# Parking seven sets of weight factors in DRAM through GpSimd's DMA queue instead of SyncE's, in a two-layer graph kernel

## Chip, cores and metric

The kernel runs on one core of one Trainium2 chip. The metric is the device time of one execution in microseconds (us). Three runs of the kernel before took 2225.2, 2225.92 and 2229.39 us; the median is 2225.92 us.

## What is computed

The input is 128 graphs of 128 nodes with 512 features each, and a 128 x 128 adjacency matrix per graph. Two layers follow each other, both with a layer norm ahead of them and a residual sum behind them.

```python
h = jnp.maximum(_layernorm(x, axis=-1), 0.0)
x = x + _L0_gnn_ref(h, adj, ...)     # attention over the edges, then three hops:
    # transition = row-normalised A * exp(leaky_relu(...))
    # for k in range(3): H += Xk @ Wk[k] + bk[k]; Xk = transition @ Xk ; relu(H)
h = jnp.maximum(_layernorm(x, axis=-1), 0.0)
x = x + _L1_gnn_ref(h, adj, nodemask, ...)
    # q, k = split(h @ Wqk); v = h @ Wv; agg = adj @ k
    # softmax over the nodes of (q . agg) / sqrt(512), times v
```

Everything is float32.

## The kernel before

**Staging.** The graphs are taken in 64 pairs p. A first loop (`for p in range(NP)`, from line 745 on) does layer 0 for all pairs and prepares layer 1; a second part, from line 842 on, does layer 1 on quads of graphs. Products with weights are done by Strassen's scheme, with seven products in place of eight block products (`strassen`, line 371), in layer 1 by two nested levels of it.

**One pass of the first loop** has, on TensorE, the seven products of `y10(p)`, the eight small products of `inner(p)` and `outer(p)` that apply the attention matrix (tile `tt`), and the seven products of `y2(p + 2)`, which belong to a later pair. Around them run:

- `load_x(p + 4)` (line 101): SyncE's queue loads the input of a later pair into `xg`. VectorE takes its statistics one pass later (line 290), ScalarE its norm.
- `outer`, line 621 and 623: VectorE adds the residual into `x1`, and SyncE's queue stores that to `x1d`. 
- `t_by_blocks` (lines 529 and 534): the attention matrix goes to DRAM (`td`) and comes back in blocks (`tv`, printed as `junk`); VectorE transposes it into `tt` for the next pass.
- `norm2` with `by_blocks` (lines 337 and 342): the normed input of layer 1 goes to `h2d` and comes back by blocks as `hv`. `for_layer1`, in the next pass, transposes `hv` into `fw` (line 427). In the second pass of each two passes it then forms two sums of it on VectorE (lines 442 and 443); in the first pass, two sums of older data (its `upper`, ahead of the transposes). GpSimd's queue stores `fw` to `fd` (line 435).
- the end of `y2` (lines 470 and 472): GpSimd's queue stores a small transposed tile to `pzd` and, once that has landed, loads it back spread over all partitions as `pz`. `pz` is used in the next pass (`attention_exp`).
- `load_adj(p + 3)` (lines 107 and 111): one load on SyncE's queue and four on GpSimd's (`agb`).

**Weights for layer 1.** Layer 1's right-hand factors need the inner level of the scheme too. In the passes p = 9 to 15 (`FIRST` = 9, seven `FACTORS`), `prepare` makes one factor a pass: four VectorE subtractions of 128 x 256 elements into a `stage` tile (line 191; two of them in `between`, two in the middle of the statistics), and `store_all`, which puts seven blocks into the DRAM tile `RWD[o]`: the four of `stage` and three that are parts of the factor itself (`rl`, later `tl`). `rightl[o][:, k, h * HD:(h + 1) * HD]` is block (k, h) of that factor. In the passes p = 16 to 19, four of the seven are read back into `RW[o]`; the other three are read by GpSimd's queue after the loop.

**What sets the order.** Each engine executes its instructions in one order, and its queue issues its DMAs in one order with the waits in between. The order is set by a planner, which may place an instruction against its place in the program (in the trace the `agb` loads of a pass stand ahead of the store to `pzd` that the program makes first); `behind(what, op, ...)` puts an instruction behind a named one, `done[what]`, in the order of the same engine. `store_all` is put behind `x1d`, so on SyncE's queue the four stores stand right behind the store of `x1` and ahead of the next `load_x`. (Through such helpers many instructions carry line 86 in the profile; they are told apart by their tiles.)

Of the kernel before, what the change touches and what calls it, by code (L numbers as in the profile page):

```python
# [16 lines left out]
def kernel(  # L17
# [25 lines left out]
    nc = tc.nc  # L43
    B, N, D = x.shape
# [5 lines left out]
    G = 2  # L50
# [26 lines left out]
    done = {}  # L77
# [5 lines left out]
    def behind(what, op, *args, **how):  # L83

        with tc.issue_after(done[what]):
            return op(*args, **how)  # L86
# [6 lines left out]
    def bcast(ap, offset, n):  # L93

        return bass.AP(tensor=ap.tensor, offset=ap.offset + offset, ap=[[0, P], [1, n]])
# [100 lines left out]
    def combined(r, t):  # L196
        return dict(zip((5, 6, 7, 4, 1, 2, 3), t + [r[0, 0], r[1, 0], r[1, 1]]))
# [124 lines left out]
    HV, LEFT, Y2, PZ, T, TT, X1, HV2, FW = ({} for _ in range(9))  # L322
# [48 lines left out]
    def strassen(banks, left, right, s, first, ends, steps={}, gate="warm", second="warm", seventh="warm"):  # L371

        w = right[1].shape[2:]
        a, b, c, e = (t[:, :w[0]] if len(w) == 1 else t for t in banks)

        def product(bank, i, start=False):
            if len(w) > 1:
                bank = bank.rearrange("p (k o) -> p k o", k=w[0])  # L380
            for k in range(HC):
                ordered(nc.tensor.matmul, bank, left[i][:, k * P:(k + 1) * P], right[i][:, k],
                        start=(start and k == 0), stop=(k == HC - 1), skip_group_check=True)
            if i in steps:
                steps[i]()

        product(a, 1, first)
        done["ba"] = behind(second, nc.scalar.copy, b, a).ins
        product(e, 5, first)
        done["s"] = behind(gate, nc.scalar.copy, s[:, 0], e).ins  # L390
        product(b, 6)
        done["u2"] = behind("s", nc.scalar.copy, c, b).ins
        product(a, 2)
        ends[0, 0](a)
        product(c, 7)
        done["s7"] = behind(seventh, nc.scalar.copy, s[:, 1], c).ins
        ends[1, 1](e, s[:, 1])
        product(b, 3)
        ends[0, 1](b, s[:, 0])
        product(c, 4)  # L400
        ends[1, 0](c)
# [45 lines left out]
    def y2(p, steps={}, gate=None, after="ln"):  # L447


        add = partial(behind, gate, nc.vector.tensor_add) if gate else nc.vector.tensor_add  # L450
        y = Y2[p] = front.tile([P, G, 2, WP], FP, name="y2")[:, :, :, :W2]
        s = front.tile([P, 2, WP * 2], FP, name="s", bufs=1)[:, :, :W2]

        def y00(a):
            done["y00"] = behind(after if gate else "warm", nc.scalar.copy, y[:, 0, 0], a).ins

        def y10(c):
            done["y10"] = nc.scalar.copy(y[:, 1, 0], c).ins

        strassen(set2, LEFT[p], right2, s, True, {  # L460
            (0, 0): y00,
            (1, 1): lambda e, t: add(y[:, 1, 1], e, t),
            (0, 1): lambda b, t: add(y[:, 0, 1], b, t),
            (1, 0): y10}, steps, seventh="y00")
        if p > 1:

            t = small.tile([P, G, S32], FP, name="pzt", bufs=1)
            behind(gate or "warm", nc.vector.transpose, t, y[:, :, 0, :S32])
            d = dram.tile([G, Q, S32], FP, name="pzd")
            nc.gpsimd.dma_start(d.rearrange("g q b -> q g b"), t[::S32])  # L470
            PZ[p] = front.tile([P, G, N], FP, name="pz")
            nc.gpsimd.dma_start(PZ[p].rearrange("p g n -> p (g n)"), bcast(d, 0, G * N))
        else:
            PZ[p] = a2[:, :G * N].rearrange("p (g n) -> p g n", g=G)

# [167 lines left out]
    rightl = {}  # L643
    RWD = {o: dram.tile([P, 7, HD], FP, name=f"rwd{o}", bufs=1) for o in FACTORS}
# [4 lines left out]
    def prepare(o, stage):  # L649

        r = {(k, h): rightl[o][:, k, h * HD:(h + 1) * HD] for k in range(2) for h in range(2)}
        t = stage.tile([P, 4, HD], FP, name="stage")

        def store_all():
            behind("x1d", nc.sync.dma_start, RWD[o][:, :4], t)
            for i, at in enumerate(((0, 0), (1, 0), (1, 1))):
                behind("x1d", nc.sync.dma_start, RWD[o][:, 4 + i], r[at])

        return combine_steps(r, [t[:, i] for i in range(4)]), store_all

# [84 lines left out]
    for p in range(NP):  # L745
        weights, weights_end = [], None
        if DC < p <= 2 * DC:
            weights = combine_steps(*OUTER)[p - DC - 1:p - DC]
            weights_end = lambda: rightl.update(combined(*OUTER))
        elif FIRST <= p < FIRST + len(FACTORS):  # L750
            weights, weights_end = prepare(FACTORS[p - FIRST], stage)

        def between():
            if p == 0:
                behind("t", norm0, 2)
                behind("rs", begin, 1)
                return
            if len(weights) > 1:
                for step in weights[:2]:
                    behind("t", step)  # L760
            if p + 2 < NP:
                behind("right" if weights else "t", begin, p + 2)
            if p + 3 < NP:
                two = weights[-2:]
                RS0[p + 3] = behind("left", statistics, xg[p + 3],
                                    middle=(lambda: [behind("aggr", step) for step in two]) if two else None, last="right")

        if p == NP - 1:
            behind("rs2", attention, p)
        def norms():  # L770
            if p and p + 3 < NP:
                behind("s7", norm0, p + 3, RS0.pop(p + 3))

        steps = {1: between, 3: norms}
        if p in T:
            steps[2] = lambda: t_transposed(p)
        if p > 1:
            steps[5] = lambda: masked(p, "ba")
        y10(p, steps)
        if p > 0:  # L780
            behind("c12", for_layer1 if p < NP - 1 else SUMS.pop(NQ - 2), *([p - 1] if p < NP - 1 else []))
        if p == NP - 2:
            f0 = w2[:, :8 * G * HC * N].rearrange("p (o j k n) -> p o j k n", o=8, j=G, k=HC)
            load_left(0, swdge)
        if p == NP - 1:
            for step in inner_sums(0, FACTORS[:4]):
                behind("c12", step)
        z = inner(p)
        if p == 0:
            y2(1, {2: lambda: RS0.update({3: behind("left", statistics, xg[3], "u2")})})  # L790
            behind("y10", behind, "hv", norm0, 3, RS0.pop(3))
            spread_columns(1)
            attention(1, lambda: begin(2))
        behind("c12" if p else "left", outer, p, z)
        if weights:
            weights_end()
        if p + 4 < NP:
            load_x(p + 4)
        if 0 < p <= DC:
            behind("x1d", rows, rl[:, :, 1], wv1, (p - 1,))  # L800
        if p == 0:
            setup_ctx.close()
            left = layer0.enter_context(tc.tile_pool(name="left", bufs=1))
            stage_ctx = ExitStack()
            stage = stage_ctx.enter_context(tc.tile_pool(name="stage", bufs=2, side="right"))
        if p + 2 < NP:
            def ahead():
                attention_exp(p + 1, gate="aggr")
                attention_adj(p + 1)

            def statistics_and_ahead():
                norm2_statistics(p, middle=ahead)
                attention_t(p + 1, "rs2")
                t_by_blocks(p + 1)

            y2(p + 2, *(({2: statistics_and_ahead}, "t", "z") if p else ()))
        if p + 2 < NP:
            behind("s7", seed_a)
            behind("s7", seed_e)
        elif p + 1 < NP:  # L820
            seeds_last()
        norm2(p)
        if p + 3 < NP:
            load_adj(p + 3)
        if p == FIRST + len(FACTORS):
            stage_ctx.close()
            prep_ctx.close()
            early = ctx.enter_context(tc.tile_pool(name="early", bufs=1, side="right"))
            RW = {o: early.tile([P, 7, HD], FP, name=f"rw{o}") for o in FACTORS[:4]}
        if FIRST + len(FACTORS) <= p < FIRST + len(FACTORS) + 4:  # L830
            o = FACTORS[p - FIRST - len(FACTORS)]
            behind("x1d", nc.sync.dma_start, RW[o], RWD[o])
    def left1(q, o, i):
        if i in INNER:
            return IN[q, o][:, INNER[i]]
# [523 lines left out]
```

## Time and profile before

| What | Value |
|---|---|
| Median of three runs | 2225.92 us |
| The profiled execution, its own time | 2229.96 us |
| Its span, first to last instruction | 2228.2 us |
| TensorE (PE) busy | 2205.7 us, 99% of the span |
| VectorE (DVE) busy | 1672.1 us, 75% |
| ScalarE (ACT) busy | 1235.8 us, 55% |
| GpSimd (POOL) busy | 698.6 us, 31% |
| Mean granted TensorE clock | 0.999 |
| Stores to `rwd` on SyncE's queue (SPq) | 28, from 260.6 to 401.9 us |
| Loads `rw<-rwd` on SyncE's queue | 4, from 427.3 to 492.3 us |
| Loads `rw<-rwd` on GpSimd's queue | 3, from 1430.4 to 1431.4 us |

Matmul ends are modelled, so a busy TensorE says only that it was fed. Idle times of TensorE in a stretch, and the distance from one pass to the next, say more. In lists of instructions each row is: line, engine, operation, tiles written and read, count, durations in ns (least, median, most), first and last start. In lists of waits each row is: who waited, for whom, us in total, how often, the longest.

### The profile page before, as it was taken

The numbers are of one execution on the slowest core, as the hardware profiler recorded it, in microseconds if no ns is written. First come the engines' busy times: TensorE is split into PE (matmuls) and PEld (weight loads), VectorE is DVE, ScalarE is ACT, GpSimd is POOL, SyncE is SP. The second block draws the span as 40 slices with busy tenths as digits, with TensorE's granted clock in tenths as the row PEclk, the third lists the DMA queues.
The fourth block names the chain that finished last, engine by engine and source line by source line (L and its number), as shares of the span: only waits on it lengthen the run. The fifth ranks groups of instructions, "written<-read, shape, count | busy, mean of one in ns | idle before, by whom it ended". The sixth has DMA issues, their size and how long they took to land.

```text
span 2228.2 us, 29421 instructions
## 1 busy us (share of the span) xinstructions
PE 2205.7 (99%) x8113; PEld 1535.0 (69%) x8113; DVE 1672.1 (75%) x4529; ACT 1235.8 (55%) x2858; POOL 698.6 (31%) x822
## 2 busy tenths in 40 slices
PE   9999999999999999999999999999999999999998
PEld 5666665656666665666666666688888878887886
DVE  5778777778787777877778787587777767777777
ACT  4555554455554555545555554456666666666664
POOL 3111111111121211212112121245555555555454
PEclk9999999999999999999999999999999999999999
DMA  7688788888787887878778786668888888888876
GB/s 208 181 243 244 230 266 248 266 271 246 225 239 222 238 238 220 244 227 232 234 227 241 218 245 211 250 205 239 223 262 226 237 223 256 235 227 242 239 219 179
DMA packets 425615, 519.35 MB, mean 233 GB/s; under 512 B 100310, under 2 KB 281174, under 8 KB 409578
## 3 DMA queue, kind: packets, MB, share of 16 engines
q1 hardware_dynamic: 383880, 391.84, 58.1%
q0 software_dynamic: 41280, 125.09, 21.6%
q8 instruction: 65, 1.06, 0.2%
q14 instruction: 100, 0.82, 0.1%
q10 hardware_dynamic: 290, 0.53, 0.1%
HBM read 295.26 MB, written 222.07 MB: 232 GB/s over the span
## 4 chain that ended last, share of the span: by engine, by line
PE 90%; DVE 4%; DMA 3%; SPq 1%; ACT 1%; issue 1%; DVEq 0%
PE a L91 26%; PE c L91 24%; PE b L91 24%; PE e L91 15%; DMA td<-t 2%; DMA hv<-h2d 1%; SPq L534 1%; DVE st L290 0%; DMA tl<-in_L_gnn_Wqk_dram 0%; DVE fw L427 0%; DVE z L86 0%; SPq L342 0%; DVE x L621 0%; DMA xg<-in_x_dram 0%; SPq L86 0%
## 5 line engine op out<-in xcount | busy, mean ns | idle before, releaser
L669 POOL TENSOR_TENSOR c<-s,c 128x512 f32<-128x512 f32 (+1 forms) x186 | 201.0, 1094 | 250.2 <-DVE s L669 244.9
L111 POOL DMA_DIRECT2D agb<-in_adj_dram x256 | 149.7, 591 | 338.8 <-DVE aT L86 251.8
L91 PE MATMUL a<-r,x 128*128 128x512 f32 x512 | 242.4, 596 | 0.1
L91 PE MATMUL b<-rw,in 128*128 128x256 f32 x884 | 212.0, 379 | 0.0
L91 PEld LDWEIGHTS b<-rw,in 128*128 128x128 f32 x884 | 168.0, 190 | 23.3 <-issue 0.5
L435 POOL DMA_DIRECT2D fd<-fw x62 | 34.7, 559 | 464.3 <-DVE fw L443 278.0
L91 PEld LDWEIGHTS a<-r,x 128*128 128x128 f32 x512 | 97.6, 191 | 96.8 <-issue 93.4
L86 ACT COPY s<-c 128x257 f32<-128x257 f32 (+1 forms) x128 | 61.5, 481 | 173.4 <-PE c L91 173.2
L86 ACT COPY b<-a 128x257 f32<-128x257 f32 (+1 forms) x128 | 59.3, 464 | 171.6 <-PE a L91 171.6
L86 DVE TENSOR_TENSOR e<-e,s 128x512 f32<-128x512 f32 x64 | 44.7, 699 | 143.5 <-ACT s L86 143.5
L669 POOL TENSOR_TENSOR c<-c 128x1024 f32<-128x1024 f32 x61 | 144.1, 2362 | 11.2 <-DVE c L669 10.9
L91 PE MATMUL a<-w,x 128*128 128x257 f32 x512 | 131.9, 380 | 0.1
L91 PE MATMUL b<-w,sx 128*128 128x257 f32 x512 | 132.0, 380 | 0.0
L91 PE MATMUL b<-t,sx 128*128 128x512 f32 x256 | 120.4, 592 | 1.2 <-ACT b L86 1.2
L91 PE MATMUL c<-t,sx 128*128 128x512 f32 x256 | 120.5, 593 | 0.2
L91 PE MATMUL b<-r,sx 128*128 128x512 f32 x256 | 120.3, 592 | 0.0
L91 PE MATMUL e<-t,sx 128*128 128x512 f32 x256 | 120.3, 592 | 0.0
L91 PE MATMUL c<-t,x 128*128 128x512 f32 x256 | 120.3, 592 | 0.0
L669 DVE SCALAR_TENSOR_TENSOR junk<-agg,wscale,c 128x512 f32<-128x512 f32 x126 | 97.1, 770 | 29.9 <-POOL c L669 24.6
L669 ACT ACTIVATE c<-c,wcol 128x512 f32<-128x512 f32 x124 | 86.3, 720 | 56.7 <-DVE wcol L669 56.7
L427 DVE STREAM_TRANSPOSE fw<-hv 128x256 f32<-128x256 f32 x248 | 88.1, 413 | 30.1 <-DMA hv<-h2d 29.7
L91 PE MATMUL a<-rw,f 128*128 128x256 f32 x448 | 108.1, 379 | 0.0
(265 smaller groups left out, 5258.1 us busy)
## 6 DMA issues: line engine op xcount, KB each, us to landing
fd<-fw POOLq DMA_DIRECT2D x62, 1024.0 KB, 5.1
x1d<-x SPq DMA_DIRECT2D x64, 512.0 KB, 4.2
h2d<-h SPq DMA_DIRECT2D x64, 512.0 KB, 3.7
xg<-in_x_dram SPq DMA_DIRECT2D x63, 512.0 KB, 7.1
hd<-h SPq DMA_DIRECT2D x63, 512.0 KB, 3.6
hv<-hd SPq DMA_DIRECT2D x252, 128.0 KB, 4.2
hv<-h2d SPq DMA_DIRECT2D x248, 128.0 KB, 4.1
h<-h2d SPq DMA_DIRECT2D x62, 512.0 KB, 8.4
```

Source lines behind the costliest of these rows:

```text
L86: return op(*args, **how)
L91: done["mm"] = op(*args, **how).ins
L111: nc.gpsimd.dma_start(agb[p][c * S32:(c + 1) * S32].rearrange("p g q i -> p (g q) i"), v[c])
L427: done["c12"] = nc.vector.transpose(blocks[:, k, j].rearrange("p f (n b) -> p f n b", n=Q), hv[:, j].rearrange("p n (k f a) -> p k f n a", ...
L435: nc.gpsimd.dma_start(fd[:, half].rearrange("p o n -> p (o n)"), fv[:, half].rearrange("p o n -> p (o n)"))
L534: done["tv"] = nc.sync.dma_start(tv[c * S32:(c + 1) * S32].rearrange("p g q i -> p (g q) i"), v[c]).ins
L669: done[engine] = op(*args, **how).ins
```

## The change

The four stores a pass become three: the blocks (1, 0) and (1, 1) lie side by side in the factor, so one store takes both. All three go through GpSimd's queue, behind the load of `pz`, which gets a name in `done` for that. The call of `store_all` moves behind `y2(p + 2)` in the program, since that `pz` load is made there. The four loads back in the passes 16 to 19 go through GpSimd's queue too, behind `pz` as well. The data moved and VectorE's subtractions stay as they are.

```diff
-            nc.gpsimd.dma_start(PZ[p].rearrange("p g n -> p (g n)"), bcast(d, 0, G * N))
+            done["pzq"] = nc.gpsimd.dma_start(PZ[p].rearrange("p g n -> p (g n)"), bcast(d, 0, G * N)).ins
...
         def store_all():
-            behind("x1d", nc.sync.dma_start, RWD[o][:, :4], t)
-            for i, at in enumerate(((0, 0), (1, 0), (1, 1))):
-                behind("x1d", nc.sync.dma_start, RWD[o][:, 4 + i], r[at])
+            behind("pzq", nc.gpsimd.dma_start, RWD[o][:, :4], t)
+            behind("pzq", nc.gpsimd.dma_start, RWD[o][:, 4], r[0, 0])
+            behind("pzq", nc.gpsimd.dma_start, RWD[o][:, 5:7].rearrange("p i d -> p (i d)"), rightl[o][:, 1])
...
         behind("c12" if p else "left", outer, p, z)
-        if weights:
-            weights_end()
         if p + 4 < NP:
             load_x(p + 4)
...
             y2(p + 2, *(({2: statistics_and_ahead}, "t", "z") if p else ()))
+        if weights:
+            weights_end()
         if p + 2 < NP:
             behind("s7", seed_a)
...
             o = FACTORS[p - FIRST - len(FACTORS)]
-            behind("x1d", nc.sync.dma_start, RW[o], RWD[o])
+            behind("pzq", nc.gpsimd.dma_start, RW[o], RWD[o])
```

## The prediction, made before the result was known

> **What bounds the kernel now.** The page first: TensorE is busy nearly throughout, so only its idle time can be won.
>
> ```profile
> PE 2205.7 (99%) x8113; PEld 1535.0 (69%) x8113; DVE 1672.1 (75%) x4529; ACT 1235.8 (55%) x2858; POOL 698.6 (31%) x822
> ```
>
> Then busy time in stretches of 50 us (after the stretch: PE, PEld, DVE, ACT, POOL, each with its count, then granted clock, DMA share, GB/s), to see where TensorE idles.
>
> ```profile
> 150.00:200.00 50.00, 50.00 (x175) 32.96 (x174) 42.31 (x133) 27.62 (x66) 10.95 (x19) 1.00 0.86 255
> ...
> 250.00:300.00 50.00, 48.92 (x161) 30.17 (x160) 38.38 (x117) 25.56 (x59) 8.14 (x14) 1.00 0.82 246
> 300.00:350.00 50.00, 47.96 (x158) 30.10 (x157) 37.29 (x120) 24.16 (x57) 8.69 (x15) 0.97 0.86 267
> 350.00:400.00 50.00, 47.72 (x164) 30.65 (x164) 38.42 (x124) 25.24 (x61) 8.13 (x14) 1.00 0.85 249
> 400.00:450.00 50.00, 48.19 (x160) 29.84 (x160) 37.31 (x122) 27.14 (x63) 11.07 (x19) 1.00 0.90 267
> 450.00:500.00 50.00, 50.00 (x161) 30.16 (x160) 36.08 (x117) 25.61 (x61) 8.73 (x15) 1.00 0.89 271
> ```
>
> The idle 7.2 us lie in 250 to 450 us, just where `rwd` is stored (260.6 to 401.9 us). The distance between passes says more, since it holds slow clock and small gaps too. Two rows of the tile `tt`, two products a pass, first for 500 to 1400 us, then for 232.3 to 502.6 us:
>
> ```profile
> L91 PE MATMUL a<-y,tt x84: 379/379/483, 502.5 to 1386.2; 128*128 128x256 f32 x84
> ```
>
> ```profile
> L91 PE MATMUL a<-y,tt x25: 379/379/483, 232.4 to 502.5; 128*128 128x256 f32 x25
> ```
>
> An undisturbed pass takes (1386.2 - 0.2 - 502.5) / 41 = 21.55 us (the last row is the second product of its pass). The twelve passes from 232.4 to 502.5 took 270.1 where 12 x 21.55 = 258.6 us were due: **11.5 us are lost**, 7.2 of them as idle TensorE. About 1.9 are slow clock: after the longest idle, 2.04 us, four `a<-r,x` products took 3.50 us against 1.88 elsewhere, with the clock at 0.56 to 0.59 from 332 to 336 us.
>
> Last the waits, from 262 to 430 us (seven passes), and from 500 to 1400 us (some 42):
>
> ```profile
> DVE st L290 <- DMA xg<-in_x_dram: 14.3, 7, 3.1
> ...
> DVE fw L427 <- DMA hv<-h2d: 12.1, 7, 2.9
> ...
> PE c L91 <- ACT s L86: 5.4, 4, 2.0
> ```
>
> ```profile
> DVE fw L427 <- DMA hv<-h2d: 12.0, 23, 1.2
> ```
>
> VectorE waits for `xg` in every pass with stores (0.7 us in two waits elsewhere) and 1.7 us a pass for `hv` (0.3 elsewhere). ScalarE's logarithm of the statistics stands ahead of the copies that TensorE needs, so VectorE's lateness reaches TensorE ("PE c <- ACT s"). SyncE's queue in the pass from 254 us shows why:
>
> ```profile
> 259.88 0.40 SPq L623 DMA_DIRECT2D x1d<-x  x1
> 260.59 0.34 SPq L86 DMA_DIRECT2D rwd<-stage  x1
> 260.98 3.00 SPq L86 DMA_DIRECT2D rwd<-rl  x3
> 264.02 0.44 SPq L101 DMA_DIRECT2D xg<-in_x_dram  x1
> 264.57 0.41 SPq L529 DMA_DIRECT2D td<-t  x1
> 265.50 0.36 SPq L337 DMA_DIRECT2D h2d<-h  x1
> ```
>
> `xg` starts 4.1 us after `x1d`; at 507.69 and 508.12 us, without stores, 0.4 us after. Behind it `td` and `h2d` are pushed too, and with them `tt` and `hv`.
>
> **What the Trainium skill says.** "DMA: Bandwidth & Descriptors", section "Issuing engines are not separate DMA queues": all queues feed the same 16 DMA engines, and another issuer saves only the sequencer's time to issue, usually small. Here it isn't small (3.34 us for the four stores above, 5.45 at 374.7 us), because the DMAs are near full then. The same page, "Queues, rings and completion order": each DMA engine takes turns between queues packet by packet; so a store on GpSimd's queue slows SyncE's transfers beside it instead of holding them up whole. No row of before shows such a pair by itself. "SBUF — State Buffer", section "SBUF: two separate sides": VectorE in a two-port mode keeps GpSimd from writing descriptors. The trace doesn't show it biting: the 62 `pz` loads took 541 to 593 ns.
>
> **The change part by part.**
>
> Removed from SyncE: four stores a pass, 3.3 to 5.5 us. `xg` then starts as early as elsewhere. That is more than VectorE's waits for it (longest 3.1), so these go; `td` and `h2d` then go when their data is there, and the waits for `tt` go. The four `rw<-rwd` loads (0.47 us each) leave SyncE's queue too, where they stood ahead of `junk<-td`: its landing was 6.2 us at most there, 1.9 at the median elsewhere. Late next is TensorE itself.
>
> What stays: VectorE's four subtractions, about 0.41 us each. The pass that begins at 232.4 us has them, but no store yet; the next begins at 254.4 us, 22.0 us later, so they cost 0.4 us. Passes in which VectorE also forms two sums behind the `hv` transposes (691 ns each) are the tight ones, and this is one; the next, with stores, lost nothing. Four such passes: 4 x 0.4 = **1.6 us stay**.
>
> Added to GpSimd: three stores a pass at about 0.56 us (a `fd` store takes 559 ns, an `rw` load there 534), 1.7 us. In the pass from 254 us `pz` is issued at 271.3 us and the next DMA of that queue, `fd`, about 281.4 us: they fit, at no cost. GpSimd waits some 5.3 us for `pzd` ahead of `pz`; the stores stand behind that wait, and nobody reads them before 427 us. If the planner lets them stand ahead of `fd` or `agb`, those come 1.7 us later; `fw` is overwritten and `agb` read a pass later, so that costs nothing either. One store less is worth 0.5 us of an idle queue: nothing.
>
> Moved: 0.9 MB a pass out of a stretch where the DMAs are full (0.90 at 569.2 to 579.2 us in an undisturbed pass) into one where they are not (0.55 at 581.2 to 589.2, 0.61 at 602.7 to 610.7 us). At the 423 GB/s of the busiest slice that I read (378 to 380 us), 0.92 MB take 2.2 us of all DMA engines; 8 us at 45% idle offer 3.6. But `hv<-h2d` runs there, and lands just when VectorE needs it (23 waits in 42 passes). Its delay is between 0 and 4.3 us (how much `junk<-td` landed later behind an `rw` load: 6.2 less 1.9); no reason excludes a little gain. I take 1.5 to 2 us, the 2.2 us of the store less what falls into idle time. Only passes with sums feel it, since there 1.4 us of transposes and 1.4 of sums stand between `hv` and the residual. The pass from 414.3 us shows the rate: a wait of 2.0 us for `hv` led to 1.2 us of idle TensorE, the pass from 502.5 us, with 0.46 us, lost nothing. I take 0.4 us for each of three such passes and 0.4 in all for the rest: **1.6 us added**.
>
> Sum: 11.5 - 1.6 - 1.6 = **8.3 us won** in the profiled execution: its span 2228.2 would be 2219.9, its own time 2229.96 would be 2221.7. The median 2225.92 is 4.04 us lower than that. Part of this may be the slow clock, which needs an idle just long enough; without it the loss is 9.6 and the gain 6.4. Between 6.4 and 8.3 I take 7.0: 2225.92 - 7.0 = **2218.9 us**.
>
> **Rivals.** A change of 0.2%, 4.5 us, is about what a measurement of this kernel can tell from none.
>
> *A, as above*, chance 0.62: 2214.4 (all 11.5 us) to 2221.4.
>
> *B, the subtractions are the greater part*, 0.26: VectorE, 1.6 us fuller a pass, is what makes it late, and the queue only adds. For it: the 0.4 us before any store, and "DVE rs" and "mv" among the releasers of ScalarE. Against it: VectorE is less busy in these stretches (37.3 to 38.4 of 50) than in 150 to 200 us (42.3), and waits for `xg`. If three quarters of the 1.6 us come through to TensorE, 1.2 us stay in each of seven passes, 8.4 of 11.5, with 3.1 won: 2222.8. In the same class falls that the planner puts the stores elsewhere on GpSimd's queue, behind `agb` and so into the full stretch again: `xg` is then slowed by sharing, about half of the loss stays, 2220 to 2223.
>
> *C, slower*, 0.10: the store takes `hv<-h2d`'s turn. With the upper bound, 4.3 us, the four passes with sums lose about 4 us each (the pass from 320.6 us, with a wait of 2.9 us for `hv`, took 4.0 us too long, slow clock included), the three others about 1.5 (4.3 less the 2.8 of slack that sums leave free): 20.5 us, and with the 1.6 of the subtractions 22.1 against 11.5 now: 2225.9 + 10.6 = 2236.5. It decides from the point where `hv` lands over some 2.5 us late. For it: `hv` is at its deadline. Against it: turns between queues, and the idle DMAs.
>
> The last 0.02 is a planner's new order that shifts other waits, no change and slower alike.
>
> **Range.** 2214.3 to 2225.0 leaves out C, the part of B that ends at no gain, and a little of A below. Faster by over 0.2%: A, 0.62. Within: B with half of the rest, 0.27. Slower: C with the other half, 0.11.
>
> **What would show it.** Right: no `rwd` on SyncE's queue, `xg` some 0.4 us behind `x1d` in all passes, VectorE's wait for `xg` near 0, the passes from 232.4 us on close to 22 us or less, TensorE idle there under 2.5 us. Wrong: the wait for `hv` above 12 us in these passes (C), or TensorE idle with `xg` in time (B).

## The result and the profile after

The changed kernel is slower: 2237.64 us, median of six runs (2236.01 to 2240.06), against 2226.3 us before, also of six (2225.2 to 2229.39). The ratio is 1.0043, with a 95% interval of 1.0033 to 1.0053. Forecast were 2218.9 us and a gain. The profiled execution took 2236.01 us with a span of 2234.2 us, 6.0 us above the span before; it is the fastest of its six, while the profiled one before (2229.96) was slower than all six of its own. The two spans are therefore closer to each other than the medians are.

On the two queues the change did what the prediction said. SyncE's queue in the pass from 254.9 us, then GpSimd's queue in the same pass:

```profile
260.37 0.41 SPq L623 DMA_DIRECT2D x1d<-x  x1
260.82 0.47 SPq L101 DMA_DIRECT2D xg<-in_x_dram  x1
264.46 0.36 SPq L529 DMA_DIRECT2D td<-t  x1
...
268.00 1.91 SPq L534 DMA_DIRECT2D junk<-td  x4
270.01 2.48 SPq L342 DMA_DIRECT2D hv<-h2d  x4
```

```profile
269.26 0.58 POOL L472 DMA_DIRECT2D pz<-pzd  x1 [2.80 <-DMA pzd<-pzt]
269.83 0.56 POOL L86 DMA_DIRECT2D rwd<-stage  x1
270.38 1.08 POOL L86 DMA_DIRECT2D rwd<-rl  x2
```

`xg` starts 0.45 us behind `x1d`, the stores stand right behind `pz`, in an idle stretch of GpSimd. Yet TensorE is starved more than before, only later. Busy time in stretches of 50 us (PE first, then the others, clock, DMA share, GB/s):

```profile
350.00:400.00 50.00, 49.04 (x165) 30.79 (x164) 40.15 (x132) 27.53 (x66) 14.23 (x25) 1.00 0.84 266
400.00:450.00 50.00, 48.25 (x157) 29.41 (x156) 36.45 (x117) 25.01 (x60) 11.40 (x20) 1.00 0.81 252
450.00:500.00 50.00, 47.50 (x151) 29.55 (x150) 34.03 (x105) 24.25 (x57) 9.20 (x16) 0.97 0.83 242
500.00:550.00 50.00, 45.34 (x145) 28.08 (x145) 33.00 (x106) 22.93 (x56) 8.13 (x14) 0.97 0.77 225
```

The last stores are issued up to 404 us and land up to 411.3 us; the four loads `rw<-rwd` are issued from 428.0 to 496.9 us. So the distance between passes is best taken in two parts: eight passes with the subtractions and stores, and five around the loads. The first product on `tt`, two rows a pass: before, for both parts, and then after, for both parts and the undisturbed rest:

```profile
L91 PE MATMUL a<-y,tt x17: 379/379/483, 232.4 to 414.3; 128*128 128x256 f32 x17
```

```profile
L91 PE MATMUL a<-y,tt x11: 379/379/483, 414.3 to 524.1; 128*128 128x256 f32 x11
```

```profile
L91 PE MATMUL a<-y,tt x17: 379/379/379, 232.9 to 409.3; 128*128 128x256 f32 x17
```

```profile
L91 PE MATMUL a<-y,tt x11: 379/379/483, 409.3 to 530.4; 128*128 128x256 f32 x11
```

```profile
L91 PE MATMUL a<-y,tt x82: 379/379/379, 530.4 to 1392.1; 128*128 128x256 f32 x82
```

An undisturbed pass is (1392.1 - 0.2 - 530.4) / 40 = 21.54 us. The eight passes lost 181.9 - 8 x 21.54 = 9.6 us before and 176.4 - 172.3 = 4.1 us after: **5.5 us won**. The five passes lost 109.8 - 107.7 = 2.1 us before and 121.1 - 107.7 = 13.4 us after: **11.3 us lost**. (The rest of the 6.0 us is small: 1.0 us was gained ahead of the first product on `tt`, and 1.4 lost in a pass at 102 us, where nothing was changed.)

The border between the two parts is not the border between stores and loads. The first of the five passes begins at 409.3 us, and its losses come from what was issued before:

```profile
402.77 0.55 POOL L86 DMA_DIRECT2D rwd<-stage  x1
402.95 3.07 SPq L342 DMA_DIRECT2D hv<-h2d  x4
403.31 1.07 POOL L86 DMA_DIRECT2D rwd<-tl  x2
```

VectorE then waits 3.8 us for that `hv`, before the first load is issued at 428.0 us, and this pass alone takes 2.0 us too long (1.6 before). In the experiments below the pass loses as much wherever the loads go (2.1 us in e1 and e4, 2.0 in e5, 1.9 in e11) and nothing where there are no stores (e8). So the stores' share of the change is better read from nine passes, 11.2 us lost before and 6.1 after, **5.1 us won**, and the loads' share from the last four, 0.5 us before and 11.4 after, **10.9 us lost**.

The waits say who is late, from 410 to 530 us (the first pass's 3.8 us for `hv` among them):

```profile
DVE fw L427 <- DMA hv<-h2d: 9.4, 5, 4.1
...
DVE tt L86 <- DMA junk<-td: 7.0, 2, 4.1
...
PE c L91 <- ACT s L86: 5.1, 2, 3.3
PE a L91 <- DVE tt L86: 3.9, 2, 2.5
```

TensorE now waits for `tt`, `tt` for `junk<-td`, and VectorE up to 4.1 us for `hv`. One such chain, in order of time:

```profile
447.20 2.75 SPq L534 DMA_DIRECT2D junk<-td  x4
447.68 0.58 POOL L472 DMA_DIRECT2D pz<-pzd  x1 [3.26 <-DMA pzd<-pzt]
448.26 0.55 POOL L86 DMA_DIRECT2D rw<-rwd  x1
450.05 2.43 SPq L342 DMA_DIRECT2D hv<-h2d  x4
...
456.60 0.45 DVE L86 STREAM_TRANSPOSE tt<-junk 128x256 f32<-128x256 f32 x1 [4.08 <-DMA junk<-td]
457.10 0.70 PE L91 MATMUL a<-y,tt 128*128 128x256 f32 x2 [2.50 <-DVE tt L86]
```

The load is issued 1.1 us after `junk<-td` began, on the other queue, and still `tt` has to wait for `junk` until 456.6 us.

### The profile page after: what moved, and what is told of

It is laid out like the page before. It is cut to its first block, busy times and chain, and to the rows that moved or that the text cites. A ratio compares the mean times of both kernels' runs of the same rounds, so it can differ in the third digit from the quotient of the medians.

```text
span 2234.2 us, 29415 instructions
## 1 busy us (share of the span) xinstructions
PE 2207.2 (99%) x8113; PEld 1536.3 (69%) x8113; DVE 1671.7 (75%) x4529; ACT 1235.4 (55%) x2858; POOL 712.1 (32%) x847
## 4 chain that ended last, share of the span: by engine, by line
PE 88%; DVE 5%; DMA 4%; ACT 1%; SPq 1%; issue 1%; DVEq 0%
PE a L91 26%; PE c L91 24%; PE b L91 23%; PE e L91 15%; DMA hv<-h2d 2%; DVE st L290 1%; DMA td<-t 1%; SPq L534 0%; DVE x L621 0%; DMA tl<-in_L_gnn_Wqk_dram 0%; SPq L342 0%; DVE z L86 0%; DVE fw L427 0%; DMA h2d<-h 0%; DMA xg<-in_x_dram 0%
## 5 line engine op out<-in xcount | busy, mean ns | idle before, releaser
L86 ACT COPY s<-c 128x257 f32<-128x257 f32 (+1 forms) x128 | 61.6, 481 | 176.5 <-PE c L91 176.4
L669 POOL TENSOR_TENSOR c<-c 128x1024 f32<-128x1024 f32 x61 | 144.1, 2362 | 11.2 <-DVE c L669 10.8
```

What stands on the lines that cost most here:

```text
L669: done[engine] = op(*args, **how).ins
```

## Experiments

**Theory L**: the stores' move wins, the loads' move loses more. A load puts 0.9 MB, in rows of 7168 bytes, into another ring of the DMA engines while SyncE's small rows of `junk` and `hv` are under way and due. **Rival S**: it is the stores that cost, by taking `hv`'s turn, as case C of the prediction has it. Under L it was further open whether the moment, the queue's kind, or the rows' size does it.

All ratios are to the kernel before, run beside. "Lost" is worked out from each profile as above, in us: the eight passes, then the five after them, then what of these five lies in their first pass, which what the last store delayed still reaches. Each loss is that of one execution. Kernels with the same stores on GpSimd's queue differ by 1.6 us in the eight passes (2.8 to 4.4) and by 1.7 us in the next (0.4 to 2.1), so a difference of some 2 us or less between two rows is not to be read as an effect.

| Kernel | Median us | Ratio (95% interval) | Lost, eight | Lost, five | In the first of the five |
|---|---|---|---|---|---|
| before | 2226.3 to 2228.43 | 1 | 9.6 | 2.1 | 1.6 |
| changed | 2237.64 | 1.0043 (1.0033 to 1.0053) | 4.1 | 13.4 | 2.0 |
| e1 stores only | 2224.23 | 0.9983 (0.9977 to 0.999) | 3.6 | 2.2 | 2.1 |
| e2 loads only | 2240.98 | 1.0058 (1.0045 to 1.0071) | 9.8 | 14.5 | 0.6 |
| e3 loads in seven slices | 2230.28 | 1.0005 (0.9995 to 1.0014) | 2.8 | 9.9 | 0.8 |
| e4 loads behind `agb` | 2226.27 | 0.9992 (0.9985 to 0.9999) | 3.6 | 4.4 | 2.1 |
| e5 loads late on SyncE | 2226.19 | 0.9989 (0.9981 to 0.9997) | 4.1 | 3.7 | 2.0 |
| e6 loads in 28 pieces, SyncE | 2222.71 | 0.9974 (0.9966 to 0.9982) | 4.4 | 0.5 | 0.4 |
| e7 all late on SyncE | 2224.34 | 0.9984 (0.9976 to 0.9993) | 1.3 | 5.0 | 1.0 |
| e8 no stores | 2221.17 | 0.9974 (0.9966 to 0.9982) | 1.6 | 0.0 | 0.0 |
| e9 late stores, 28 pieces | 2220.77 | 0.9971 (0.996 to 0.9983) | 2.5 | 0.5 | 0.2 |
| e10 loads on ScalarE | 2232.51 | 1.0022 (1.0009 to 1.0034) | 3.5 | 11.2 | 1.5 |
| e11 28 pieces, GpSimd | 2224.08 | 0.9989 (0.9982 to 0.9996) | 4.0 | 1.8 | 1.9 |

**e1, one part alone: the stores.** Against the changed kernel:

```diff
-            behind("pzq", nc.gpsimd.dma_start, RW[o], RWD[o])
+            behind("x1d", nc.sync.dma_start, RW[o], RWD[o])
```

> The stores go through GpSimd's queue as in the changed kernel, the four loads stay on SyncE's queue behind the store of x1 as before. Theory L (the four loads on GpSimd's queue cost more than all the rest brings): the eight passes with stores lost 9.5 us before and lose 4.1 after, the five passes around the loads lost 2.1 before and lose 13.4 after; so this kernel should be about 5.4 us faster than before, 2219 to 2223 us. Theory S (the stores take hv's turn on the DMA engines, case C of the prediction): still slower than before, 2230 us or more.

Faster than before by 0.17%, by its median 1.2 us above theory L's range. Theory S falls as the cause of the slowdown. The stores are not free, though: 3.6 + 2.1 = 5.7 us are lost in the nine passes, where 1.6 are lost without any store (e8). The four loads, back on SyncE's queue, lose 0.1 us in the last four passes.

**e2, the other part alone: the loads.** Against the kernel before:

```diff
-            nc.gpsimd.dma_start(PZ[p].rearrange("p g n -> p (g n)"), bcast(d, 0, G * N))
+            done["pzq"] = nc.gpsimd.dma_start(PZ[p].rearrange("p g n -> p (g n)"), bcast(d, 0, G * N)).ins
...
-            behind("x1d", nc.sync.dma_start, RW[o], RWD[o])
+            behind("pzq", nc.gpsimd.dma_start, RW[o], RWD[o])
```

> Only the four loads move to GpSimd's queue, behind the pz load; the stores stay on SyncE's queue. Theory L: about 11 us slower than before, 2235 to 2239 us. Theory S: no change to before within 2 us.

Slower by 0.58%, about 13 us, some 2 us beyond the range. Four DMA instructions do all of the harm.

**e3, smaller rows at the same moment.** Against the changed kernel:

```diff
-            behind("pzq", nc.gpsimd.dma_start, RW[o], RWD[o])
+            for i in range(7):
+                behind("pzq", nc.gpsimd.dma_start, RW[o][:, i], RWD[o][:, i])
```

> The changed kernel, with each of the four loads cut into seven DMAs of 1 KB a partition, on the same queue at the same place. Theory H (a DMA engine takes the load's rows of 7168 bytes in long turns, and SyncE's rows of 128 bytes wait for whole turns): smaller rows give SyncE's transfers their turns back, and most of the 13.4 us around the loads go: 2222 to 2229 us. Theory B (only the bytes count that stand in the way at this moment): as slow as the changed kernel, 2235 to 2240 us.

Just above H's range, and far from B. In its profile `junk` was free again (landing 4.1 us at most, 8.4 in the changed kernel), but `hv` wasn't, VectorE waiting 13.8 us for it in four passes: seven DMAs one after the other stay in the way longer (from 446.1 to 456.1 us, where the single load took from 448.3 to 455.5). One thing makes this a weaker test of row size than it was meant to be. In the DMA records of the trace, the slices on GpSimd's queue do not appear as rows of 1024 bytes but as 896 records of 4096 bytes, four rows in each. So 4096 bytes were compared with 7168. That the shorter records freed `junk`, and the bytes still held up `hv`, fits this run; pieces of 1024 bytes in another ring at this moment were not tried.

**e4, another moment on the same queue.** Against the changed kernel:

```diff
-            nc.gpsimd.dma_start(agb[p][c * S32:(c + 1) * S32].rearrange("p g q i -> p (g q) i"), v[c])
+            done["agbq"] = nc.gpsimd.dma_start(agb[p][c * S32:(c + 1) * S32].rearrange("p g q i -> p (g q) i"), v[c]).ins
...
-            behind("pzq", nc.gpsimd.dma_start, RW[o], RWD[o])
+            behind("agbq", nc.gpsimd.dma_start, RW[o], RWD[o])
```

> The changed kernel, with the four loads on GpSimd's queue directly behind the agb loads, some 6 us earlier in the pass than behind pz. Theory M (it is the moment: behind pz the load meets the reads of td and h2d that the next pass waits for): the load is done before those start, and the time falls to 2220 to 2226 us. Theory Q (the queue itself, wherever the load stands in the pass): 2232 us or more.

The moment takes 9 of the 13.4 us away; the median is 0.3 us above M's range. Issued about as early as SyncE's queue had the loads before (11.1 to 14.5 us into the pass; 11.3 to 13.0 there), they still lose 2.3 us in the last four passes, against 0.5 there. The 1.8 us between them are too few to be read from single executions.

**e5, the late moment on SyncE's queue.** Against the changed kernel:

```diff
-            behind("pzq", nc.gpsimd.dma_start, RW[o], RWD[o])
+            behind("hv", nc.sync.dma_start, RW[o], RWD[o])
```

> Stores through GpSimd's queue as in the changed kernel; the four loads on SyncE's queue, behind the issue of the last hv<-h2d load, about 17 us into the pass, so as late as the changed kernel has them, but in the ring of the transfers that they met. Theory M (the late moment alone): as slow as the changed kernel, 2235 us or more. Theory R (a late load on another ring takes turns with transfers that were issued before it, while on the same ring those go first): no loss for td and hv, 2219 to 2224 us.

Between the two, and far from M: 3.7 us lost, not 13.4, and 2.0 of them in the pass of the last store. The landing of `junk<-td` from 405 to 530 us, first in the changed kernel, then here:

```profile
DMA to landing us min/median/max: 1.9/2.7/8.4
```

```profile
DMA to landing us min/median/max: 1.7/2.1/3.9
```

The loads go out later than on GpSimd's queue (18.0 to 20.6 us into the pass, 15.4 to 18.6 there), so the two differ in the moment too. The first load is the closest pair: issued 18.6 us into its pass on GpSimd's queue, 19.4 us on SyncE's, it is followed by a pass that lost 2.7 us there and nothing here. In the same ring, the load does not overtake what was issued ahead of it. The other 1.7 us of the 3.7 lie in the last two passes and were not taken apart.

**e6, the same bytes in 28 passes.** Against the changed kernel:

```diff
-        if FIRST + len(FACTORS) <= p < FIRST + len(FACTORS) + 4:
-            o = FACTORS[p - FIRST - len(FACTORS)]
-            behind("pzq", nc.gpsimd.dma_start, RW[o], RWD[o])
+        if FIRST + len(FACTORS) <= p < FIRST + len(FACTORS) + 28:
+            n, i = divmod(p - FIRST - len(FACTORS), 7)
+            o = FACTORS[n]
+            behind("x1d", nc.sync.dma_start, RW[o][:, i], RWD[o][:, i])
```

> Stores through GpSimd's queue; each load cut into seven of 1 KB a partition, one a pass over 28 passes, on SyncE's queue behind the store of x1. Theory L: what the loads still cost on SyncE's queue in the kernel with only the stores moved (2.2 us in the five passes from the sixteenth on) goes, 128 KB a pass being nothing beside some 4.8 MB: 1 to 2 us faster than that kernel, 2218 to 2223 us. Rival: 28 more SyncE issues behind x1d push xg by 0.4 us each and cost as much as they save.

The time is in L's range, and the rival's cost for `xg` isn't seen. But L's reason isn't shown: the 2.2 us that the pieces were to save lie almost all (2.1) in e1's pass of the last store, ahead of its first load, and that the same pass lost only 0.4 us here has nothing to do with the loads. The intervals of e1 and e6 overlap as well.

**e7, stores behind `hv` on SyncE's queue.** Against the changed kernel, with the call of `store_all` moved behind `norm2(p)` and the loads as in e5:

```diff
-            behind("pzq", nc.gpsimd.dma_start, RWD[o][:, :4], t)
-            behind("pzq", nc.gpsimd.dma_start, RWD[o][:, 4], r[0, 0])
-            behind("pzq", nc.gpsimd.dma_start, RWD[o][:, 5:7].rearrange("p i d -> p (i d)"), rightl[o][:, 1])
+            behind("hv", nc.sync.dma_start, RWD[o][:, :4], t)
+            behind("hv", nc.sync.dma_start, RWD[o][:, 4], r[0, 0])
+            behind("hv", nc.sync.dma_start, RWD[o][:, 5:7].rearrange("p i d -> p (i d)"), rightl[o][:, 1])
```

> Stores (three a pass) and loads all on SyncE's queue, behind the issue of the last hv<-h2d load instead of behind the store of x1. Theory R: the ring's own order protects junk and hv, what follows (the store to hd and its way back) has time: 2217 to 2222 us, faster than with the stores on GpSimd's queue. Theory M: the stores now hold up hd and hv<-hd, the passes lose 1 to 2 us each: 2226 us or more.

By its median the kernel lies between the two ranges. The eight passes lost 1.3 us, the least of any kernel with stores, and the next one 1.0; the loads, even later here, took 4.1 in the last four. SyncE's queue in the pass from 254.7 us:

```profile
269.66 1.93 SPq L342 DMA_DIRECT2D hv<-h2d  x4
271.91 0.34 SPq L86 DMA_DIRECT2D rwd<-stage  x1
272.31 1.41 SPq L86 DMA_DIRECT2D rwd<-rl  x2
```

Three stores take 1.81 us of the queue here, in a gap; four took 3.4 ahead of `xg`.

**e8, the subtractions by themselves.** `store_all` is empty and the loads of e6, and those after the loop, read a layer-0 weight instead:

```diff
-            behind("pzq", nc.gpsimd.dma_start, RWD[o][:, :4], t)
...
+            pass
```

> Leaves out the stores to RWD; the factors' loads read the layer-0 weights instead, in 28 pieces of the same size on SyncE's queue and three whole ones after the loop, so layer 1 computes with other weights. VectorE's subtractions stay. Theory A (prediction: the subtractions alone cost 0.4 us in every second pass): the passes 9 to 16 lose 1.6 us, 2216 to 2220 us. Theory B (the subtractions are the greater part of the loss): the passes lose 4 us or more, 2220 us or more, no faster than the kernel with the stores and the same loads.

The passes lost 1.6 us, 0.41 in each of four, as theory A has it; the median is 1.2 us above A's range. By time the kernel can't be told from e6, which has the same loads and the stores (0.9974 each), so the case against B rests on the passes of one execution. The waits from 230 to 410 us show who:

```profile
PEld c L91 <- ACT c L86: 3.9, 4, 1.0
...
DVE fw L427 <- DMA hv<-h2d: 2.8, 4, 1.2
```

Four times, ScalarE's copy into `c` stands behind a logarithm that waits for VectorE's later statistics.

**e9, the two best halves.** The stores of e7 and the loads of e6.

> The two best halves together: three stores a pass on SyncE's queue behind the last hv<-h2d load (the passes with stores lost 1.3 us so, against 4.1 on GpSimd's queue), and the loads in 28 pieces on SyncE's queue behind the store of x1 (0.4 us lost). Theory R: 1.7 us lost in all where the kernel before lost 11.6; 2216 to 2220 us, the fastest of all, ratio 0.995 to 0.997. Rival: the gain of the late stores was bought by the passes after them, and the sum is no better than with the stores on GpSimd's queue: ratio 0.9974 as there.

The lowest ratio of all, 0.9971, just above R's range, but its interval holds that of e6. The late stores lost 2.5 us here, not 1.3. In the nine passes it is 2.7 us here and 2.3 in e7, against 3.6 to 6.1 in the kernels with stores on GpSimd's queue. That late stores on SyncE's queue beat those is likely, not shown.

**e10, a third ring.** Against the changed kernel, the load goes out in the next pass:

```diff
-            behind("pzq", nc.gpsimd.dma_start, RW[o], RWD[o])
...
+        if FIRST + len(FACTORS) < p <= FIRST + len(FACTORS) + 4:
+            o = FACTORS[p - FIRST - len(FACTORS) - 1]
+            steps[7] = lambda: behind("ln", nc.scalar.dma_start, RW[o], RWD[o])
```

> The changed kernel with its four loads on ScalarE's queue, behind the second activation of the statistics, some 15 us into the pass: about the moment of the changed kernel, a third ring, and descriptors that GpSimd doesn't write. Theory R (any other ring takes turns with SyncE's small rows, with 7168 bytes a turn): about as slow as the changed kernel, 2232 us or more, junk<-td landing up to 6 us late. Theory G (it is GpSimd's own way of issuing): no more loss than with late loads on SyncE's queue, 2223 to 2228 us; ScalarE's time to issue adds 1 to 2 us to either.

In R's range: 11.2 us lost, 1.5 of them in the first pass, and the same waits; the landing of `junk<-td` from 405 to 530 us:

```profile
DMA to landing us min/median/max: 1.7/3.0/8.3
```

So it isn't GpSimd's way of issuing: both other rings that were tried do it. Packets started per microsecond, counted from the DMA records of this trace while a load ran (SyncE's queue had issued all four `hv` by 472.1 us, so its rows were waiting):

```
us           7168 B, ScalarE's ring   512 B, SyncE's ring
472 to 473   53                       46
473 to 474   28                       28
474 to 475   18                       20
475 to 476   7                        379
```

In the first three of these, a row of `hv` of 512 bytes (27 to 36 ns) goes out about once for each row of 7168 bytes (286 to 324 ns). The rings take turns, and the small rows get an eighth to a twentieth of their later pace. (In the second and third, GpSimd's ring started 12 and 15 rows of 4096 bytes as well.) For `junk`'s rows of 128 bytes in the changed kernel the shares vary more: from 449 to 453 us 16, 1, 19 and 215 of them started in a microsecond, beside 5, 15, 45 and 46 of 7168 bytes.

**e11, pieces on GpSimd's queue.** As e6, but behind `pzq` on GpSimd's queue.

> The changed kernel with its four loads cut into 28 pieces of 128 KB, one a pass, on GpSimd's queue at the same place behind pz. Theory P (the harm grows with the bytes that stand in other rings at once, not with the queue): as with the pieces on SyncE's queue, 2219 to 2224 us. Theory G: each pass loses a part of a us, 28 passes, 2230 us or more.

Just above P's range by its median. In the five passes 1.8 us are lost, all in the pass of the last store; the four after it lose nothing, against 11.4 us with whole loads at the same place. (In the records the pieces have 4096 bytes here, as in e3, and 1024 on SyncE's queue in e6.) The ratio is 0.15% above e6's, with intervals that touch.

## Why the prediction was wrong

**The gain it saw is there.** The stores ahead of `xg` cost what it said: the nine passes lost 11.2 us with them on SyncE's queue and 1.6 without stores (e8), which is 9.6 us where the prediction had 11.5 - 1.6 = 9.9. Also right: GpSimd has the room (three stores in a stretch that was idle), VectorE's wait for `xg` goes, and the subtractions leave 1.6 us.

**The step that failed is the loads.** "They leave SyncE's queue too, where they stood ahead of `junk<-td`" counted them as a gain, and "0.4 in all for the rest" was all that their new place was given. They lost 11.4 us in four passes, 10.9 more than before and twice what the stores won (e2, which moves them alone, loses 13.9 there). Two errors lie in it. The prediction looked for the DMA engines' free time only for the stores, and gave the loads the same place unpriced, though a load is as many bytes, in rows nearly twice as long as the stores' longest (7168 against 4096 bytes). And it took from the turns between rings that a transfer on another queue slows SyncE's "instead of holding them up whole". The turns are there (e10), but a turn holds a long row on one side and about one short row on the other, so small rows beside large ones nearly stand still. In SyncE's own ring what was issued earlier is safe (e5). Behind `pz` the load meets just the two transfers that the next pass waits for; 4 to 7 us earlier on the same queue it loses 2.3 us (e4).

**The stores' meeting with `hv` was sized too small, by nearly three times.** "1.6 us added" stood for it. Measured are 6.1 - 1.6 = 4.5 us in the nine passes of the changed kernel, and 4.1 in e1. The prediction counted three passes with sums at 0.4 us; four met a delayed `hv`, and beyond the subtractions they lost 1.1, 0.3, 1.1 and 2.0 us. So the stores' move alone wins some 5 us in the passes and 0.17%, about 4 us, in time (e1), not 8.3 and 7.0. The prediction's own signs show this, from 262 to 430 us in the changed kernel:

```profile
DVE fw L427 <- DMA hv<-h2d: 12.2, 6, 3.8
```

That is above the 12 us that were to mean case C (a weak sign, since it was 12.1 before the change), and TensorE is idle for 4.1 us from 250 to 450 us, where under 2.5 were to mean A. Both came out in between: the stores do take time from `hv`, but less than they free.

**Rival C had the right time by the wrong cause.** Its 2236.5 us is within 1.2 us of the median, with the range's upper end at 2225.0. That is luck: it laid 22 us on the stores, which won, and nothing on the loads. Its landing delay of 4.3 us was taken as an upper bound from a window that ended at 430 us, so from the first of the four loads alone; behind the third, `junk<-td` landed after 7.7 us in the kernel before. In the changed kernel it is 8.4. A late landing alone isn't the loss either: before, with landings up to 7.7 us, the four passes lost 0.5 us, since the loads went out and were done earlier in the pass.

## What to carry to other kernels

When DMAs move to another queue to clear the way for a critical one, price each where it lands: which small-row transfers are under way or due there, how many bytes the mover brings at once and how long its rows are. Here, a transfer put behind the critical ones in their own ring did not overtake them (e5), and one ahead of them held them up (the stores before); in another ring it slowed them wherever it met them (the changed kernel, e10). When a large transfer that nobody waits for has to go out beside them in another ring, cut it into pieces over many passes: on GpSimd's queue, behind `pz`, 28 pieces lost nothing in the four passes where the whole loads lost 11.4 us. Early on SyncE's queue whole loads lost next to nothing (e1: 0.1 us), and a gain from cutting isn't shown there.

## What the runs showed of the hardware

- Between rings the DMA engines went about row by row: 46 rows of 512 bytes to 53 of 7168 in a microsecond, where 512-byte rows went at 379 once the load was nearly through. "DMA: Bandwidth & Descriptors", section "Queues, rings and completion order" of the Trainium skill has turns by packet, typically some 9 to 17 descriptors; this trace shows about one row a turn.
- A record of the trace is one row on SyncE's and ScalarE's rings, but up to 4096 bytes of shorter rows on GpSimd's. The same pieces of 128 KB with rows of 1 KB make 128 records of 1024 bytes in e6 (SyncE) and 32 records of 4096 bytes in e11 (GpSimd).
- GpSimd's time to issue was the same for rows of 1 KB and of 7 KB: 0.54 to 0.56 us a DMA. SyncE's varied from 0.34 to 1.47 us for the store of `stage` alone. Long issues came with full DMAs, though full DMAs didn't always bring them. Counted from the trace of before, from 100 to 1390 us, 125 of the 467 DMAs that SyncE issued while the DMA share was 0.9 or more took over 0.7 us to issue, and only 18 of the other 688.
- TensorE's clock fell behind some long idles. In the changed kernel, three stretches from 512 us:

```profile
512.00:516.00 4.00, 0.70 (x3) 0.29 (x2) 3.83 (x17) 1.80 (x6) 0.69 (x2) 0.97 1.01 362
516.00:520.00 4.00, 4.00 (x8) 2.25 (x8) 3.90 (x16) 2.37 (x5) 2.14 (x4) 0.60 1.02 309
520.00:524.00 4.00, 4.00 (x11) 1.76 (x10) 2.85 (x11) 2.44 (x7) 0.70 (x2) 1.00 0.59 155
```

After 3.30 us of idle the clock was 0.60 for 4 us, and four products of 128 x 257 took 2.06 us where such four took 1.03 ahead of it. In the kernel before, 2.04 us of idle did the same: four `a<-r,x` products took 3.50 us instead of 1.88. Such a wait cost some 1.6 to 1.8 us beyond its own length. But the idle's length alone doesn't decide. In e2 the clock stayed at 1.00 after 3.03 us of idle, and in e3 after 2.22 us that ended at 463.5 us. From e2, the product that ended the wait and the stretch from 300 us:

```profile
300.26 0.70 PE L91 MATMUL a<-y,tt 128*128 128x256 f32 x2 [3.03 <-DVE tt L86]
```

```profile
300.00:304.00 4.00, 3.74 (x17) 3.33 (x18) 3.84 (x10) 1.49 (x4) 0.56 (x1) 1.00 0.78 250
```
